# The input half of a GRU's new gate by Strassen's scheme, the state half as loose filler, and a new table of exchanges, on one Trainium2 core

## The chip, the cores and the metric

The kernel runs on one core of one Trainium2 chip. The core has a matrix engine (TensorE, PE in the profile; PEld is its weight load), a vector engine (VectorE, DVE), an activation engine (ScalarE, ACT), GpSimd (POOL) and a sync engine (SyncE, SP). PE multiplies a tile of weights by a tile of data into a PSUM bank; DVE and ACT read and write both PSUM and on-chip memory; SP and POOL issue most of the DMA transfers. Each engine takes its instructions in a fixed order and waits on semaphores. A queue of transfers is held up as well while the transfer at its head waits.

The metric is device time in microseconds (us) for one execution. Before the change: 2009.32 us, the median of three runs (2005.86 to 2010.85).

## The reference, cut to what matters

For 32 graphs of 512 nodes with 256 features everything is float32:

```python
h = max(layernorm(x), 0)                                # per graph [512, 256]
c = relu(bn1(conv1x1(h^T)))                             # 256 -> 256 channels
x_conv = relu(bn2(conv17(c)) + h^T)^T                   # 17 taps along the nodes
s = h @ w_se^T + b_se;  A = exp(-dist(s)) * adj         # [512, 512], s has 3 columns
x_nmp = A @ relu(h @ w_msg^T + b_msg)
gi = [x_conv, x_nmp] @ w_ih^T + b_ih                    # 512 -> 768
gh = h @ w_hh^T + b_hh                                  # 256 -> 768
r = sigmoid(gi_r + gh_r);  z = sigmoid(gi_z + gh_z)
n = tanh(gi_n + r * gh_n)
out = x + (1 - z) * n + z * h
```

The matrix products fill the time: the 17-tap convolution (already turned into 25 smaller products per group of columns by a transform of data and weights), the two products of the graph, and the gate products above. The change is about the gate products, the transform of the convolution's data, and the line with `w_msg` and `w_se`.

## The kernel before, in words

The work is five streams written as Python generators: `rows` (1x1 convolution), `begins` (layer norm and turning of a graph), `graphs` (messages, kernel matrix, masked product), `conv` (the 17-tap convolution in 7 groups of columns, 25 products each) and `gates` (one call of `gates(b)` per graph b). A small planner at the end of the kernel steps the streams. It keeps a model of each engine's time. A stream yields the planner's time at which its next step can go, or a condition; among the streams that can go the planner takes the one that lies furthest behind its share. The table `OTHERS` names choices, by their running number, at which it takes the second or third of the able streams instead. So the order of the instructions on all engines is fixed when the kernel is built, by the planner's constants and by this table. Work for DVE and ACT that isn't urgent goes through `later(t, f)`, a list by due time; `settle()` issues the whole list at once.

All matrix instructions are issued at line 259, all DVE, ACT and most POOL work at line 241, all transfers at line 228. Tiles tell the work apart: `ps_acc` (three PSUM banks) belongs to the gates, `ps_g` to graph and rows, `ps_c` to the convolution.

**The gates before.** For a graph b there are three gates (r, z, n), each with 256 output features in two halves o = 0, 1 of 128. The three data tiles with 2 x 128 input features on the partitions and 512 nodes are `hTb` (state), `xconv` and `xnb` (inputs); each has two buffers. For graphs 1 to 30 the gates r and z are made together by Strassen's scheme in Winograd's form (7 products in place of 8, on half tiles): 2x2 blocks are the two gates by the two halves of input features on one side, and the two halves of 256 nodes on the other. The sums of the weights are made once (`weight_sums`, tiles `wsum`), those of the data per graph by DVE (`data_sums`, tiles `t`). For each o that is 7 products of three sources, each 128 x 256. Two partial results must be copied or added between PSUM banks on the way (ACT's copies, and DVE's adds in `spread`: `ps_acc<-ps_acc,r`, 128 x 256). The new gate isn't in this scheme: per o there are two state products (`hidden`: `ps_acc<-hTb,whh`, 128 x 512) and four input products (`new`, 128 x 512). ACT halves the state part and adds its bias in PSUM, DVE multiplies it there by (tanh + 1) (`ps_acc<-r,ps_acc`), and the input products are then summed on top of it in the same bank. These last products are put into the next unit's waits by `some_new`.

After that comes the mix of a unit: ACT makes n (`r<-ps_acc,vec`), DVE does three operations of 128 x 512 into a tile `o_sb` and `r`, transposes `r` into `o_sb`, and POOL adds `o_sb` onto the output in DRAM by four transfers (`out_dram<-o_sb`). SP has copied x to the output before. Graph 0 and graph 31 (`PLAIN`) are done without the scheme. In the last part of the program, after the other streams have ended, the gates are alone.

**The message step before** (`messages`): per quarter of the nodes one product of 259 columns (256 of `w_msg`, 3 of `w_se`), and two DVE adds that take the bias and leave PSUM, one of 256 and one of 3 columns. `factors` builds from the 3 columns the two small factors of the kernel matrix.

**The transform before** (`fives_alone`): for each group of columns but the first, DVE makes five combinations of the convolution's input in 12 long operations of about 128 x 1632.

## Time and profile before

| | |
|---|---|
| median of 3 runs | 2009.32 us |
| profiled execution, first to last instruction | 2013.5 us |
| PE busy | 1973.8 us, 98% |
| DVE busy | 1505.0 us, 75% |
| ACT busy | 874.1 us, 43% |
| POOL busy | 478.5 us, 24% |
| mean granted clock of PE | 0.991 |
| first gate product, last convolution product, last product outside the gates | 253.5, 1816.4, 1835.1 us |

Each executed float32 product appears in the trace as two matrix instructions, so a count of the trace is twice the count of the program (a few records are missing). The duration of one matrix instruction in the trace holds its way through the array; the pace at which PE goes through them is read from the starts of neighbouring rows. A bracket at the end of a row of the timeline gives the idle time before it and what ended it.

### The profile page before, as it was taken

What the parts mean: (1) busy time and instruction counts of PE and PEld (TensorE: products, weight loads), DVE (VectorE), ACT (ScalarE), POOL (GpSimd) and SP (SyncE); (2) the same over time, 40 slices, a digit from 0 to 9 for tenths busy, and PEclk for the clock granted to TensorE, in tenths of its full rate; (3) what the DMA queues carried; (4) which work ended last, traced back from release to release, by engine and by line L of the source; (5) the groups of instructions that cost most, each with busy time, mean ns of one, the idle gap of its engine ahead of it and who ended that gap; (6) DMA issues with size and microseconds to landing.
All of it is one profiled execution on the core that took longest, in us unless ns stands there. A gap on an engine that the chain in (4) does not pass through costs nothing.

```text
span 2013.5 us, 28526 instructions
## 1 busy us (share of the span) xinstructions
PE 1973.8 (98%) x9692; PEld 1450.8 (72%) x9692; DVE 1505.0 (75%) x2711; ACT 874.1 (43%) x1755; POOL 478.5 (24%) x628
## 2 busy tenths in 40 slices
PE   8999999999999999999999999999999999999998
PEld 5887666776778677776787776777776777776774
DVE  6889589976988597876787775688894877766443
ACT  6644463434634455333464235463334453324321
POOL 3222112222212132222231221232220221113232
PEclk9999899999999999999999999999999999999999
DMA  8446777888898788889787886798895876665564
GB/s 295 168 174 211 238 241 194 211 209 197 227 252 208 194 191 213 200 195 222 146 235 192 204 202 162 191 246 203 179 211 150 185 171 155 157 151 106 111 100 34
DMA packets 578177, 378.92 MB, mean 188 GB/s; under 512 B 457664, under 2 KB 475488, under 8 KB 576896
## 3 DMA queue, kind: packets, MB, share of 16 engines
q1 hardware_dynamic: 419760, 279.15, 49.7%
q0 software_dynamic: 157184, 97.81, 26.4%
q8 instruction: 77, 1.26, 0.2%
q14 instruction: 68, 0.56, 0.1%
q10 hardware_dynamic: 1088, 0.13, 0.0%
HBM read 278.94 MB, written 114.56 MB: 195 GB/s over the span
## 4 chain that ended last, share of the span: by engine, by line
PE 65%; DVE 4%; issue 2%; DMA 1%; ACT 1%; POOL 1%; DVEq 0%; POOLq 0%; SPq 0%; ACTq 0%
PE ps_acc L259 36%; PE ps_c L259 16%; PE ps_g L259 13%; DVE o_sb L241 1%; DMA cd<-part 1%; PE ps_g L265 1%; DVE t L241 0%; POOL out_dram L228 0%; DVE x L241 0%; DMA hd<-hT 0%; POOL cd L228 0%; DVE ps_acc L241 0%; ACT at L241 0%; DVE z L241 0%; DMA w<-wd 0%
## 5 line engine op out<-in xcount | busy, mean ns | idle before, releaser
L228 POOL DMA_DIRECT2D out_dram<-o_sb x252 | 275.8, 1719 | 636.5 <-DVE o_sb L241 510.9
L259 PEld LDWEIGHTS ps_c<-xd,w 128*128 128x128 f32 x2304 | 285.5, 190 | 49.9 <-ACT ps_c L241 33.9
L259 PEld LDWEIGHTS ps_c<-x,w 128*128 128x128 f32 x2032 | 259.8, 194 | 48.2 <-issue 32.9
L259 PE MATMUL ps_c<-xd,w 128*128 128x135 f32 (+1 forms) x2304 | 290.4, 279 | 3.9 <-ACT ps_c L241 3.9
L259 PE MATMUL ps_c<-x,w 128*128 128x135 f32 (+2 forms) x2032 | 268.5, 281 | 2.8 <-DVE x L241 2.8
L259 PE MATMUL ps_g<-at,msg 128*128 128x512 f32 x512 | 230.0, 600 | 3.5 <-DVE at L241 3.5
L241 DVE TENSOR_TENSOR ps_acc<-ps_acc,r 128x256 f32<-128x256 f32 x120 | 51.7, 431 | 230.4 <-PE ps_acc L259 209.3
L259 PE MATMUL ps_acc<-hTb,whh 128*128 128x512 f32 (+2 forms) x532 | 211.4, 495 | 1.4 <-ACT r L241 1.4
L259 PE MATMUL ps_acc<-xconv,wih 128*128 128x512 f32 (+2 forms) x532 | 211.6, 495 | 0.7 <-DVE ps_acc L241 0.7
L259 PE MATMUL ps_acc<-xnb,wih 128*128 128x512 f32 (+2 forms) x532 | 209.1, 496 | 3.2 <-DVE ps_acc L241 3.2
L259 PEld LDWEIGHTS ps_g<-at,msg 128*128 128x128 f32 x512 | 96.9, 193 | 112.8 <-issue 103.4
L259 PE MATMUL ps_acc<-t,wsum 128*128 128x256 f32 x720 | 175.7, 380 | 1.2 <-DVE wsum L241 1.2
L259 PEld LDWEIGHTS ps_acc<-t,wsum 128*128 128x128 f32 x720 | 135.7, 191 | 35.5 <-issue 17.9
L259 PEld LDWEIGHTS ps_acc<-xconv,wih 128*128 128x128 f32 x532 | 98.0, 190 | 48.3 <-issue 38.6
L259 PE MATMUL ps_g<-hT,w 128*128 128x512 f32 (+8 forms) x296 | 124.5, 571 | 7.4 <-DMA hT<-hd 6.8
L259 PEld LDWEIGHTS ps_acc<-xnb,wih 128*128 128x128 f32 x532 | 96.1, 190 | 44.8 <-issue 31.5
L259 PE MATMUL ps_g<-wmsg,hTg 128*128 128x259 f32 x496 | 124.4, 382 | 0.0
L259 PE MATMUL ps_acc<-t,wih 128*128 128x256 f32 x480 | 123.2, 380 | 0.0
L259 PEld LDWEIGHTS ps_acc<-hTb,whh 128*128 128x128 f32 x532 | 94.7, 190 | 38.5 <-issue 28.3
L241 DVE TENSOR_TENSOR x<-x 128x544 f32<-128x544 f32 (+2 forms) x175 | 120.2, 707 | 0.3
L241 ACT ACTIVATE ps_c<-ps_c 128x270 f32<-128x270 f32 (+1 forms) x144 | 56.3, 391 | 137.9 <-PE ps_c L259 137.7
L241 ACT ACTIVATE h<-ps_g,bn_shift,bn_scale 128x252 f32<-128x252 f32 (+8 forms) x212 | 86.3, 484 | 60.4 <-PE ps_g L259 60.4
(157 smaller groups left out, 3251.3 us busy)
## 6 DMA issues: line engine op xcount, KB each, us to landing
w<-wd SPq DMA_DIRECT2D x414, 256.0 KB, 4.0
m_sb<-in_adj_dram SPq DMA_DIRECT2D x384, 64.0 KB, 3.4
wd<-w POOLq DMA_DIRECT2D x74, 256.0 KB, 3.3
hT<-hd SPq DMA_DIRECT2D x33, 512.0 KB, 4.0
hd<-hT POOLq DMA_DIRECT2D x32, 512.0 KB, 6.1
hTb<-hd SPq DMA_DIRECT2D x32, 512.0 KB, 4.6
xnb<-nd SPq DMA_DIRECT2D x64, 256.0 KB, 3.3
out_dram<-o_sb POOLq DMA_DIRECT2D x252, 64.0 KB, 4.8
```

The costliest lines, as they stand in the source:

```text
L228: self.engine.dma_start(dst, src, **more)
L241: getattr(self.engine, op)(*tiles, **more)
L259: nc.tensor.matmul(ps, lhsT, rhs, **more)
L265: nc.tensor.transpose(ps, a, ident)
```

## The change

The change does the following.

- **New gate by the scheme.** For graphs 1 to 30 the input products of the new gate (sources `xconv` and `xnb`) go by the same scheme, with the two halves o = 0, 1 of the outputs as the two block rows. A third run of it follows the two for r and z, with its own sums of weights `nsum`: 7 products of two sources, 128 x 256, in place of 8 products of 128 x 512. All three runs now go through one function, `scheme`.
- **State products as fill-in.** The state products of the new gate are cut into 128 x 256 and put on a list (`state`, `SPARE`), from which `spare_some` takes them into the waits inside a scheme and `spare_all` takes the rest before a scheme's last products. They have a bank of their own. DVE multiplies them by (tanh + 1) into `r`, and a new DVE add (`r<-ps_acc,r`, 128 x 512) joins them with the input products before the tanh.
- **Buffers.** `o_sb` is gone: the mix works in `hTb` itself, so the transfers to the output read `hTb`. `z` has two buffers. Some data sums are made in place in `xconv` and `xnb`, so that these have two DVE operations of 128 x 256 where one of 128 x 512 was.
- **Shorter transform.** `fives_alone` makes its five combinations in 10 long operations in place of 12 (other linear combinations of the same outputs of earlier steps).
- **One message add.** The product has 261 columns (two columns of zeros, so that bias alone gives -0.5), and one DVE add of 261 columns replaces the adds of 256 and 3.
- **Table and constants.** The least time of a matrix product in the planner's model goes from 0.2145 to 0.2235, the gates' starting clock from 1.8 to 2.0, and `OTHERS` is another table: 27 entries before, 205 now.

```diff
-        on_pe(ps, [lhsT, rhs], (0.2675 if few else max(0.2145, 0.005 + elements(ps) / 600.0)) + 0.1 * (few != narrow))
+        on_pe(ps, [lhsT, rhs], (0.2675 if few else max(0.2235, 0.005 + elements(ps) / 600.0)) + 0.1 * (few != narrow))
...
         settle_stores()
+        if ISSUED["out"] < ND * (b - 1):
+            settle()
         HB[b] = late.tile([P, ND, N], F32, name="hTb", bufs=2)
...
         for steps in (
             ((minus, 3, 1),),
-            ((minus, 2, 0), (less2, None, 3), (minus, None, 1)),
-            ((minus, 3, 1), (less2, None, 4), (minus, None, 2)),
-            ((minus, 2, 1), (less2, None, 3), (minus, None, 2)),
-            ((minus, 3, 2), (less2, 1, None)),
+            ((times(2.0), 0, None), (times(-2.0), 2, None)),
+            ((times(-2.0), 3, 4), (times(2.0), 1, None), (minus, None, 2)),
+            ((times(-3.0), 2, 3), (times(2.0), 1, None)),
+            ((minus, 3, 2), (times(-2.0), 1, None)),
         ):
...
-        dve.tensor_tensor(msg[:, c, :], ps[:, :D], bmsg[:, :D], op=ALU.add)
-        dve.tensor_tensor(gr.aug[:, c, :3], ps[:, D:], bmsg[:, D:], op=ALU.add)
+        dve.tensor_tensor(msg[:, c, :], ps, bmsg, op=ALU.add)
...
+            def scheme(ks, given, summed, temp, first, last, over=None):
+                yield bank_read
+                ps0 = acc.tile([P, N], F32, name="ps_acc")
...
+                ps1 = acc.tile([P, N], F32, name="ps_acc")
+                act.activation(ps1[:, lo], ps0[:, lo], AF.Copy)
+                copy_at = act.free + LAG
                 yield now
...
+                term(ps0[:, hi], summed(0), summed_t(0), ks)
+                fifth = temp()
+                act.activation(fifth, ps0[:, hi], AF.Copy)
+                yield from spare_some(copy_at)
                 yield copy_at
+                term(ps1[:, lo], summed(1), summed_t(1), ks)
...
+                dve.tensor_tensor(ps0[:, hi], ps1[:, lo], fifth, op=ALU.add)
+                r_at = dve.free + LAG
                 yield now
+                term(ps0[:, lo], given(1, 0), part_of(1, lo), ks)
+                yield from spare_some(r_at)
                 yield r_at
+                term(ps1[:, lo], given(0, 1), third, ks)
+                dve.tensor_tensor(ps1[:, hi], ps1[:, lo], fifth, op=ALU.add)
+                z_at = dve.free + LAG
...
+                term(ps0[:, hi], summed(2), part_of(1, hi), ks, end=True)
+                first(ps0)
...
+                yield from spare_all()
+                yield max(z_at, *(T_AT[b, 2, k] for k in ks))
+                term(ps1[:, lo], given(1, 1), summed_t(2), ks, end=True)
...
+                last(ps1)
...
+                    def add():
+                        UNREAD.discard(ps.tensor.name)
+                        dve.tensor_tensor(r[o], ps, r[o], op=ALU.add)
+                        later(dve.free + 0.2, squash)
...
+        def make_r(o):
+            settled("mix", ND * (b - 1) + o + 1)
+            r[o] = late.tile([P, N], F32, name="r", bufs=2)
...
     OTHERS = {
-        6: 1, 41: 1, 259: 1, 374: 1, 430: 1, 443: 1, 547: 1, 953: 1, 979: 1, 1020: 2,
...
+        8: 1, 11: 1, 57: 1, 67: 2, 94: 1, 100: 1, 108: 1, 135: 1, 162: 1, 178: 1, 188: 1, 199: 1,
...
```

What the change moves is seen in the order of the built programs. First PE, in the last part of the program where the gates are alone: the new gate's products for o = 0 of graph 29 before (bank 13954; the rows of bank 13979 between them begin the r and z scheme of o = 1).

```order
L259 MATMUL ps_acc_13954<-hTb_13858,whh_2263 128x512 x2
...
L259 MATMUL ps_acc_13979<-hTb_13858,whh_2263 128x256
L259 MATMUL ps_acc_13979<-xconv_13866,wih_2264 128x256
L259 MATMUL ps_acc_13979<-xnb_13813,wih_2264 128x256
L259 MATMUL ps_acc_13954<-xconv_13866,wih_2264 128x512 x2
...
L259 MATMUL ps_acc_13954<-xnb_13813,wih_2264 128x512 x2
```

And the run of the new gate for graph 29 now (banks 14383 and 14386 hold o = 0 and o = 1; 14410 takes the next graph's state products).

```order
L259 MATMUL ps_acc_14383<-xconv_14201,wih_2238 128x256
L259 MATMUL ps_acc_14383<-xnb_14242,wih_2238 128x256
L259 MATMUL ps_acc_14383<-t1_0_2246,nsum_2242 128x256
L259 MATMUL ps_acc_14383<-t2_0_2249,nsum_2242 128x256
L259 MATMUL ps_acc_14386<-t1_1_2247,nsum_2242 128x256
L259 MATMUL ps_acc_14386<-t2_1_2250,nsum_2242 128x256
...
L259 MATMUL ps_acc_14383<-xconv_14201,nsum_2242 128x256
L259 MATMUL ps_acc_14383<-xnb_14242,nsum_2242 128x256
L259 MATMUL ps_acc_14410<-hTb_14336,whh_2237 128x256 x4
L259 MATMUL ps_acc_14386<-t1_2_2248,wih_2238 128x256
L259 MATMUL ps_acc_14386<-t2_2_2251,wih_2238 128x256
```

Twelve products of 128 x 512 per graph have become 14 of 128 x 256 and 8 of 128 x 256, and in this part the state products all stand just before the last two products of a run.

Second DVE, at the step from graph 28 to graph 29 in the same part, before: the mix of one unit, the data sums of the next graph among it, up to the step on which the waiting input products rest (`ps_acc<-r,ps_acc`).

```order
L241 TENSOR_TENSOR o_sb_13891<-hTb_13739,r_13827 128x512
L241 SCALAR_TENSOR_TENSOR o_sb_13891<-z_13851,o_sb_13891 128x512
L241 SCALAR_TENSOR_TENSOR r_13827<-o_sb_13891,r_13827 128x512
L241 TENSOR_TENSOR t0_0_2268<-hTb_13858 128x512
L241 TENSOR_TENSOR t2_0_2274<-xnb_13813 128x512
L241 STREAM_TRANSPOSE o_sb_13891<-r_13827 128x512
L241 TENSOR_TENSOR t1_0_2271<-xconv_13866 128x512
L241 TENSOR_TENSOR t2_1_2275<-xnb_13813,t2_0_2274 128x256
L241 SCALAR_TENSOR_TENSOR ps_acc_13901<-r_13881,ps_acc_13901 128x512
```

The same step now: the last two data sums for graph 29, the add of o = 1, the mixes of both units of graph 28 one after the other, both transposes, and then the first add between banks of graph 29's first run.

```order
L241 TENSOR_TENSOR t1_2_2248<-xconv_14201,t1_1_2247 128x256
L241 TENSOR_TENSOR t2_2_2251<-xnb_14242,t2_1_2250 128x256
L241 TENSOR_TENSOR r_14212<-ps_acc_14249,r_14212 128x512
L241 TENSOR_TENSOR hTb_14062<-hTb_14062,r_14176 128x512
L241 SCALAR_TENSOR_TENSOR hTb_14062<-z_14196,hTb_14062 128x512
L241 SCALAR_TENSOR_TENSOR r_14176<-hTb_14062,r_14176 128x512
L241 TENSOR_TENSOR hTb_14062<-hTb_14062,r_14212 128x512
L241 SCALAR_TENSOR_TENSOR hTb_14062<-z_14238,hTb_14062 128x512
L241 SCALAR_TENSOR_TENSOR r_14212<-hTb_14062,r_14212 128x512
L241 STREAM_TRANSPOSE hTb_14062<-r_14176 128x512
L241 STREAM_TRANSPOSE hTb_14062<-r_14212 128x512
L241 TENSOR_TENSOR ps_acc_14286<-ps_acc_14294,r_14313 128x256
```

Both units' mixes and transposes now stand on DVE ahead of the next graph's first add between banks; before, one unit's mix stood there and the other's came a unit later.

Third SP, in the middle of the program: the loads around the state tile of graph 19, `hTb_11023`, now (the `w` tiles are the convolution's weights, `xconv` the same graph's convolution result).

```order
L228 DMA w_11011<-wd14_282 128x512
L228 DMA w_11013<-wd14_282 128x512
L228 DMA hTb_11023<-hd19_96 128x1024
L228 DMA xconv_11025<-cd19_152 128x1024
L228 DMA w_11037<-wd15_283 128x512
```

The load of `hTb` stands in SP's queue with the convolution's weights behind it, as before; what it must wait for is new, since the buffer that it fills is read by the transfers of graph 17's output.

More of the change, by code (lines that the diff above doesn't have):

```diff
@@ new lines, with hidden_half, hide_some, run @@
+    ISSUED = {"mix": 0, "out": 0}
+    UNREAD, STATE, SPARE, HIDE, R_AT = set(), {}, [], [], {}
+    def hidden_half(ps, o, s=slice(0, N)):
+        act.activation(ps[:, s], ps[:, s], AF.Identity, bias=bn[:, o : o + 1], scale=0.5)
+    def hide_some():
+        def run():
+            while HIDE and HIDE[0][:2] in STATE:
+                HIDE.pop(0)[2]()
+        later(act.free + 0.3, run)
+    def state(b, o):
+        def one(n):
+            i, half = divmod(n, 2)
+            if n == 0:
+                ps = STATE_PS[b, o] = acc.tile([P, N], F32, name="ps_acc")
+                UNREAD.add(ps.tensor.name)
+            ps = STATE_PS[b, o]
+            at = slice(HALF * half, HALF * half + HALF)
+            matmul(
+                ps[:, at], whh[:, i, 2 * D + o * P : 2 * D + (o + 1) * P], HB[b][:, i, at],
+                start=(n == 0), stop=(i == ND - 1), skip_group_check=True,
+            )
+            if n == 2 * ND - 1:
+                hidden_half(ps, o)
+                STATE[b, o] = ps
+                hide_some()
+        SPARE.extend((b, lambda n=n: one(n)) for n in range(2 * ND))
```

601 lines of the change are left out of this document (289 added, 312 removed), and 21 rows, old and new, of the table OTHERS.

## The prediction

> **What bounds the kernel now.** I read the page's busy times first, then PE's busy time by stage, then what stands in PE's way in the last stage.
>
> ```profile
> PE 1973.8 (98%) x9692; PEld 1450.8 (72%) x9692; DVE 1505.0 (75%) x2711; ACT 874.1 (43%) x1755; POOL 478.5 (24%) x628
> ```
>
> ```profile
> 0.00:60.00 60.00, 52.94 (x206) 33.43 (x207) 38.93 (x121) 38.58 (x84) 17.02 (x41) 0.94 0.71 261
> 60.00:340.00 280.00, 271.39 (x1599) 204.60 (x1598) 230.97 (x422) 140.37 (x304) 62.08 (x108) 0.98 0.67 210
> 340.00:1000.00 660.00, 651.42 (x3243) 483.18 (x3242) 531.11 (x946) 290.99 (x601) 152.97 (x197) 0.99 0.84 204
> 1000.00:1700.00 700.00, 694.10 (x3393) 517.17 (x3392) 531.60 (x931) 305.70 (x594) 163.52 (x200) 1.00 0.81 192
> 1700.00:1843.00 143.00, 141.93 (x689) 105.54 (x688) 102.16 (x169) 47.05 (x97) 30.67 (x32) 1.00 0.65 140
> 1843.00:2013.50 170.50, 162.04 (x572) 106.91 (x570) 70.21 (x125) 51.37 (x78) 52.20 (x52) 0.99 0.57 90
> ```
>
> The rows give stage, length, then busy time of PE, PEld, DVE, ACT, POOL, and PE's clock. PE is the bound in every stage: it idles 31.2 us in the first 1843 us (7.1 + 8.6 + 8.6 + 5.9 + 1.1) and 8.5 us in the last stage, most of these after its last product. So work taken off PE is time, as long as the new order doesn't open waits.
>
> The last stage is different in kind. From 1843 us the gates are alone, and no other stream fills a wait. Its chain of waits, in order of time:
>
> ```profile
> 1886.80 23.14 PE ps_acc L259 x86
> ...
> 1910.30 0.69 DVE o_sb L241
> ...
> 1912.35 1.29 DVE t L241 x2
> ...
> 1915.16 0.61 DVE ps_acc L241
> 1915.82 23.13 PE ps_acc L259 x86
> ```
>
> Once per graph (1886.80 to 1915.82: 29.02 us) the chain leaves PE and goes through 5.5 us on DVE (1910.30 to 1915.82), the mix of the finished unit with data sums in between, until DVE gives PE a bank back. PE's own rows show how much of this isn't covered:
>
> ```profile
> 1857.77 1.98 PE L259 MATMUL ps_acc<-xnb,wih 128*128 128x512 f32 x4 [0.98 <-DVE ps_acc L241]
> 1886.80 1.99 PE L259 MATMUL ps_acc<-xnb,wih 128*128 128x512 f32 x4 [0.30 <-DVE ps_acc L241]
> ...
> 1944.85 1.98 PE L259 MATMUL ps_acc<-xnb,wih 128*128 128x512 f32 x4 [0.30 <-DVE ps_acc L241]
> ```
>
> **The change part by part.** *Products.* The pace of PE:
>
> ```profile
> 1960.91 1.46 PE L259 MATMUL ps_acc<-t,wsum 128*128 128x256 f32 x6
> 1962.20 0.60 PE L259 MATMUL ps_acc<-hTb,whh 128*128 128x256 f32 x2
> ...
> 1976.06 3.60 PE L259 MATMUL ps_acc<-hTb,whh 128*128 128x512 f32 x8
> 1979.49 1.88 PE L259 MATMUL ps_acc<-xconv,wih 128*128 128x512 f32 x4
> ```
>
> Six instructions of 256 columns take 1.29 us from start to start, so a product (two instructions) takes 0.430 us; eight of 512 take 3.43 us, 0.8575 us a product. A graph's new gate goes from 12 x 0.8575 = 10.29 us to 22 x 0.430 = 9.46 us. Over 30 graphs that is 360 x 0.8575 - 660 x 0.430 = 308.7 - 283.8 = 24.9 us less. The messages' 256 products get two more columns of 0.43/256 us each: +0.9 us. Together **-24.0 us** of PE work, all of it on the path.
>
> *DVE and ACT.* Row by row:
>
> ```profile
> L241 DVE TENSOR_TENSOR ps_acc<-ps_acc,r 128x256 f32<-128x256 f32 x120 | 51.7, 431 | 230.4 <-PE ps_acc L259 209.3 <-ACT r L241 11.5 <-PE ps_g L265 5.1
> L241 DVE SCALAR_TENSOR_TENSOR ps_acc<-r,ps_acc 128x512 f32<-128x512 f32 x63 | 43.4, 689 | 17.0 <-ACT r L241 12.8 <-ACT ps_acc L241 4.2
> L241 DVE TENSOR_TENSOR t<-xconv,t 128x256 f32<-128x256 f32 x60 | 25.0, 416 | 0.0
> L241 DVE TENSOR_TENSOR t<-xconv 128x512 f32<-128x512 f32 x30 | 20.1, 670 | 0.0
> L241 DVE TENSOR_TENSOR aug<-ps_g,bmsg 128x3 f32<-128x3 f32 x128 | 19.3, 151 | 0.0
> L241 DVE TENSOR_TENSOR x<-x,h 128x1632 f32<-128x1632 f32 x12 | 22.3, 1855 | 0.2
> ```
>
> Added: 60 adds between banks (60 x 0.431 = 25.9 us), 60 joins `r<-ps_acc,r` (no such row; nearest is the multiply that also reads a bank, 0.689: 41.3 us), and 60 sums of 512 columns become 120 of 256 (60 x (2 x 0.416 - 0.670) = 9.7 us). Removed: 128 adds of 3 columns (19.3 us), and 2 long operations in each of 6 groups (12 x 1.855 = 22.3 us). DVE gains about 35 us, 1505 to 1540, and ACT 60 copies of 0.38 us. Both stay below PE, so in the first 1843 us I cost them at nothing: the planner sees their backlog and gives PE another stream's products meanwhile. If that cover were gone, the 35 us would be an upper price.
>
> *The last stage.* There the cover is gone, and I follow the step from one graph to the next in the order that the change builds. Time 0 is the end of graph b's last product. DVE may write the last two data sums of graph b+1 only then, since that product reads their old contents; the starts of DVE's rows at this place before give the paces:
>
> ```profile
> 1911.01 0.69 DVE L241 SCALAR_TENSOR_TENSOR o_sb<-z,o_sb 128x512 f32<-128x512 f32 x1
> 1911.74 0.69 DVE L241 SCALAR_TENSOR_TENSOR r<-o_sb,r 128x512 f32<-128x512 f32 x1
> 1912.35 0.69 DVE L241 TENSOR_TENSOR t<-hTb 128x512 f32<-128x512 f32 x1
> ...
> 1916.01 0.42 DVE L241 TENSOR_TENSOR t<-xnb,t 128x256 f32<-128x256 f32 x1
> 1916.35 0.42 DVE L241 TENSOR_TENSOR t<-xconv,t 128x256 f32<-128x256 f32 x1
> ```
>
> 0.34 us for a sum of 256, 0.73 for an operation of 512 that needs the one before it, 0.61 for one that doesn't. So: the sums from 0.15 on, the join for o = 1 at 0.83, the first mix at 1.44, 2.17, 2.90, the second at 3.51, 4.24, 4.97, the transposes at 5.58 and 6.2, and only then, at 6.8, the first add between banks of graph b+1, done by 7.25. PE reaches the product that needs this add's bank after 12 products, at 12 x 0.430 = 5.16 us. It waits about 2.1 us. Four such steps have nothing but gates around them (into graphs 27 to 30): +8.4 us, and the four waits above (0.98 once and 0.30 three times, 1.9 us) go: **+6.5 us**. Ends: -1.9 if DVE gets through in time after all, +13.3 if each wait also costs a window of half clock (below).
>
> The clock is what makes a wait dear elsewhere:
>
> ```profile
> 198.00:202.40 4.40, 1.47 (x6) 0.82 (x5) 4.23 (x13) 0.00 (x0) 0.00 (x0) 1.00 0.74 230
> 202.40:205.80 3.40, 3.40 (x6) 1.34 (x5) 0.57 (x1) 0.87 (x2) 0.00 (x0) 0.50 0.92 292
> ```
>
> ```profile
> 201.76 4.51 PE L259 MATMUL ps_g<-hT,w 128*128 128x512 f32 x6 [2.94 <-DMA hT<-hd]
> 455.69 6.71 PE L259 MATMUL ps_g<-hT,w 128*128 128x512 f32 x8 [2.33 <-DMA hT<-hd]
> 174.07 3.80 PE L259 MATMUL ps_c<-x,w 128*128 128x116 f32 x32 [1.75 <-DVE x L241]
> ```
>
> After the wait of 2.94 us PE's clock is halved for 3.4 us, which costs 1.7 us more (the last column of a stage row but two is the clock); after the one of 1.75 us the trace shows no half clock. The wait of 2.1 us that I expect lies between them, nearer the harmless one, so I take no clock loss. The Trainium skill ("TensorE: Matmul & The Clock Gate", Part 1) says that the gate goes back to half rate after at least one idle window of about 3.4 us; by that rule none of the four waits could halve the clock, while the trace's 2.94 us already did. By the rule the term stays +6.5, with the loss it would be +13.3.
>
> *The table.* The order of the first 1843 us is drawn anew. Its 31.2 us of idle PE bound the gain; a third more of it, 10 us, is my bound for a loss. The two waits for `hT<-hd` above, with a half window behind the first and two behind the second (3.4/2 + 6.8/2), are worth 10.4 us and belong to this order alone; the new order loses them and draws others. I take a little under half: **-4 us**.
>
> The sum: -24.0 + 6.5 - 4.0 = -21.5 us. The profiled execution spans 2013.5 us, 4.2 over the median, and would come to 1992; of the runs' median, 2009.3, **1988 us** is left.
>
> **The rivals.** *The last stage runs through.* DVE is in time there and the table gains more (-24.0 - 1.9 - 8): 1975 us. For it: DVE is busy only 70 of the last 170.5 us. Against it: the chain above already runs through DVE once per graph, with less in the way.
>
> *The gain goes into new waits in the middle.* Each graph has three runs with two hand-overs to ACT and two to DVE each, where it had two; if each of 26 graphs in the middle waits once more, as long as the longest wait above (0.98 us), that is +25 us against the table's -4: 2009.3 - 24.0 + 6.5 + 25 - 4 = 2013, and with half of it 2000. For it: DVE is 80% busy from 340 to 1000 us (531 of 660). Against it: in the same stage PE now loses only 1.3%.
>
> *SP is held by the state tile.* This is the way to a slower kernel.
>
> ```profile
> 1943.57 4.33 POOL L228 DMA_DIRECT2D out_dram<-o_sb x4 [11.43 <-DVE o_sb L241]
> ```
> ```profile
> out_dram<-o_sb POOLq DMA_DIRECT2D x252, 64.0 KB, 4.8
> ```
> ```profile
> SPq L228 <- PE ps_c L259: 445.8, 200, 11.3
> ```
> ```profile
> L259 PE MATMUL ps_c<-xd,w x2304: 276/279/384, 249.9 to 1816.4; 128*128 128x135 f32 x128, 128*128 128x136 f32 x64
> ```
>
> The load of `hTb` for graph b+1 fills the buffer that eight output transfers of graph b-1 read. POOL needs 2 x 4.33 us to issue them, and the last lands some 4.8 us after its issue began; with about 6 us of mix that is 19 us after graph b-1's last product, and the load stands in SP's queue after graph b's first run, 21 products or 9.0 us of PE work, some 17 us where the gates have about half of PE. So SP may stand for a few us, with the weights of the convolution behind it. They have slack: SP waits 445.8 us in all for PE to free their buffers, 2.2 us each time. It decides from the point where SP stands longer than a convolution product's period: the 150 of groups 2 to 7 lie between 250 and 1816 us, 10.4 us each; 1.5 us over that in 27 graphs would be +40: 2028 us. Against it: that needs twice the hold that I work out.
>
> *Half clock in the last stage.* Four windows, +6.8: 1995 us, still faster. *The products don't get cheaper*: excluded by the pace rows; 256 columns cost half of 512.
>
> **How the numbers follow.** The forecast (1980 to 1997) has 0.55, the last stage that runs through 0.15, waits in the middle 0.16, SP's hold 0.07, the half clock 0.07. The range takes the forecast's, most of the faster rival and the milder half of the waits: 1973 to 2005 us. A measurement of this kernel can tell 0.3%, 6 us, from no change. Faster, below 2003.3: 0.55 + 0.15 + 0.07 + a third of the waits' 0.16 = 0.82; the same 0.11; slower, above 2015.3, 0.07.
>
> **What would show it.** PE's busy time falls by 20 to 26 us. In the last stage the period of a graph is 29.5 to 30 us (27.6 of products), and PE's row of `ps_acc<-t,whh` in a run's fifth group carries a wait of about 2 us put down to DVE `ps_acc`. DVE is near 1540 us. PE's idle time before that stage is 20 to 35 us. I'd be wrong if the period there is near 27.7 (no wait), if PE waits for weights `w<-wd` in the middle (SP's hold), or if DVE's waits appear all over the middle.

## The result, and the profile after

The change makes the kernel slower: **2145.9 us** (median of 4 runs, 2141.2 to 2152.2) against 2007.6 us (4 runs) for the kernel before on the same chip, a ratio of 1.070 (95% interval 1.067 to 1.073). The prediction was 1988 us. Its profiled execution spans 2150.4 us, 136.9 more than before.

PE is still the engine with the most to do, but it no longer has a busy line without holes. The page's busy times:

```profile
PE 1996.3 (93%) x10291; PEld 1564.9 (73%) x10291; DVE 1549.5 (72%) x2747; ACT 896.3 (42%) x1815; POOL 474.9 (22%) x629
```

PE idles 154.1 us of the span, where it idled 39.7 us. By stage (columns as in the prediction: stretch, length, then busy time of PE, PEld, DVE, ACT, POOL, and PE's clock):

```profile
340.00:1000.00 660.00, 617.04 (x3262) 488.08 (x3259) 514.92 (x904) 288.38 (x599) 136.92 (x185) 0.99 0.80 198
1000.00:1700.00 700.00, 648.02 (x3310) 518.95 (x3310) 503.71 (x871) 287.91 (x567) 152.38 (x191) 0.98 0.77 179
1943.00:2150.40 207.40, 176.84 (x699) 133.05 (x697) 84.12 (x156) 53.52 (x88) 55.62 (x54) 0.96 0.51 79
```

From 340 to 1700 us PE idled 14.5 us before and idles 94.9 us now. That is where other streams have work, and where the forecast counted on no waits. The view of what PE waited for (us in total, times, longest us) names two rows that hold 125 us of it:

```profile
PE ps_acc L259 <- ACT ps_acc L241: 69.0, 68, 10.3
PE ps_acc L259 <- DVE ps_acc L241: 56.0, 55, 3.4
PE ps_g L259 <- DMA hT<-hd: 3.5, 3, 2.1
```

Before, all rows of this view came to 33.1 us and the row for DVE `ps_acc` to 4.2 us; now they come to 146.9. The groups of instructions by line (the last columns are the idle time just before a group and what ended it) tell which products stand behind these waits:

```profile
L259 PE MATMUL ps_acc<-hTb,whh 128*128 128x256 f32 x720 | 200.2, 391 | 36.5 <-DVE ps_acc L241 36.4
L259 PE MATMUL ps_acc<-t,wsum 128*128 128x256 f32 x720 | 178.4, 390 | 50.3 <-ACT ps_acc L241 50.3
L259 PE MATMUL ps_acc<-xconv,wih 128*128 128x256 f32 x540 | 166.5, 390 | 19.6 <-DVE ps_acc L241 19.6
L259 PE MATMUL ps_acc<-t,nsum 128*128 128x256 f32 x240 | 63.5, 401 | 18.7 <-ACT ps_acc L241 18.7
```

`t,wsum` and `t,nsum` begin the second group of a run of `scheme`, `hTb,whh` and (in the run of the new gate) `xconv,wih` the fourth. So it is not the fifth group that waits, the one that the prediction spoke of. One step of the last stage in order of time, rows of PE, ACT and DVE:

```profile
2046.55 0.43 DVE L241 TENSOR_TENSOR t<-xconv,t 128x256 f32<-128x256 f32 x1 [0.40 <-PE ps_acc L259]
...
2046.78 0.59 PE L259 MATMUL ps_acc<-hTb,whh 128*128 128x256 f32 x2
...
2047.32 0.68 DVE L241 TENSOR_TENSOR r<-ps_acc,r 128x512 f32<-128x512 f32 x1
...
2047.64 0.59 PE L259 MATMUL ps_acc<-xnb,wih 128*128 128x256 f32 x2
2047.92 0.68 DVE L241 TENSOR_TENSOR hTb<-hTb,r 128x512 f32<-128x512 f32 x1
2048.27 0.37 ACT L241 ACTIVATE ps_acc<-ps_acc 128x256 f32<-128x256 f32 x1 [0.80 <-PE ps_acc L259]
...
2048.69 2.86 PE L259 MATMUL ps_acc<-t,wsum 128*128 128x256 f32 x12 [0.46 <-ACT ps_acc L241]
...
2052.03 1.30 DVE L241 STREAM_TRANSPOSE hTb<-r 128x512 f32<-128x512 f32 x2
2052.82 0.38 ACT L241 ACTIVATE r<-ps_acc 128x256 f32<-128x256 f32 x1 [3.56 <-DVE hTb L241]
...
2053.25 0.43 DVE L241 TENSOR_TENSOR ps_acc<-ps_acc,r 128x256 f32<-128x256 f32 x1
...
2053.73 0.70 PE L259 MATMUL ps_acc<-hTb,whh 128*128 128x256 f32 x2 [2.18 <-DVE ps_acc L241]
...
2054.26 0.59 PE L259 MATMUL ps_acc<-xconv,wih 128*128 128x256 f32 x2
...
2054.70 0.59 PE L259 MATMUL ps_acc<-xnb,wih 128*128 128x256 f32 x2
...
2060.93 2.86 PE L259 MATMUL ps_acc<-t,wsum 128*128 128x256 f32 x12 [0.46 <-ACT ps_acc L241]
...
2064.38 0.70 PE L259 MATMUL ps_acc<-hTb,whh 128*128 128x256 f32 x2 [0.59 <-DVE ps_acc L241]
```

The first group ends in the left half of a bank. ACT copies that half into another bank (2048.27 to 2048.64), and only then PE goes on, though its next product needs nothing of the copy: it writes the right half of the same bank. The second wait is the same with DVE: the add writes the right half (2053.25 to 2053.68), and the product behind it, whose sum goes into the left half, starts at 2053.73. In the program's list of PE's instructions both products carry a wait, one for ACT and one for DVE. Here are the second to fourth group of a run late in the program, of the change and of the kernel before (numbers of tiles left out):

```
change                                  before
ps_acc<-t_0,wsum [waits Activation]     ps_acc<-t_0,wsum [waits Activation]
ps_acc<-t_0,wsum                        ps_acc<-t_0,wsum
ps_acc<-t_0,wsum                        ps_acc<-t_0,wsum
ps_acc<-t_1,wsum [waits DVE]            ps_acc<-hTb,whh
ps_acc<-t_1,wsum                        ps_acc<-xconv,wih
ps_acc<-t_1,wsum                        ps_acc<-xnb,wih [waits DMAHW0]
ps_acc<-hTb,whh [waits DVE]             ps_acc<-t_1,wsum [waits DVE,PE]
ps_acc<-xconv,wih                       ps_acc<-t_1,wsum [waits DVE]
ps_acc<-xnb,wih                         ps_acc<-t_1,wsum
```

Before, the product of the left half came ahead of ACT's second copy and of the add, so it had nothing to wait for. The wait for ACT's first copy was there as well, but new-gate products from a list stood between the first group and the second. In the trace of the kernel before, same place in the last stage:

```profile
1914.92 0.59 PE L259 MATMUL ps_acc<-xnb,wih 128*128 128x256 f32 x2
1915.82 1.98 PE L259 MATMUL ps_acc<-xnb,wih 128*128 128x512 f32 x4 [0.30 <-DVE ps_acc L241]
1917.64 1.88 PE L259 MATMUL ps_acc<-xconv,wih 128*128 128x512 f32 x4
1919.36 1.46 PE L259 MATMUL ps_acc<-t,wsum 128*128 128x256 f32 x6
```

The rows of the trace leave the numbers of the tiles out. Laid beside the program's list, which has them, no row of PE in the whole trace of the change overlaps in time with a row of ACT or DVE on the same PSUM tile. The Trainium skill ("PSUM — Partial Sum Buffer", section "PSUM bank collisions raise a hardware error") says that two engines may not touch the same bank in the same partitions at once, at disjoint columns either, and that the compiler's scheduler therefore puts a dependency between them. The trace agrees with the dependency; what would happen without it was not tried.

The price of such a hand-over, from the rows: where nothing waits, pairs start 0.43 to 0.44 us apart (2054.26, 2054.70). From 2047.64 to 2048.69 are 1.05 us, 0.62 more. The wait in the bracket is 0.46 of it; the rest is the way of PE's last product out of the array before ACT can begin. The first pair after a wait takes 0.10 us more (2053.73 to 2054.26: 0.53). A copy thus costs 0.72 us. From 2060.93 to 2064.38 are 3.45 us for six products (2.58), 0.10 of the excess from the wait ahead of them; with the pair behind it the add costs 0.87 us.

Not every hand-over costs only that. In the last stage the bare wait is 0.46 us for a copy and 0.59 us for an add. Cut at these two lengths, the 123 waits of the two rows hold 63 us; the other 62 us are time in which ACT or DVE, busy with other work, came late to the copy or add (the longest wait is 10.3 us). This split is an estimate from the single waits of the two rows.

### The profile page after: what moved, and what is told of

It is laid out like the page before. It is cut to its first block, busy times and chain, and to the rows that moved or that the text cites. A ratio compares the mean times of both kernels' runs of the same rounds, so it can differ in the third digit from the quotient of the medians.

```text
span 2150.4 us, 29846 instructions
## 1 busy us (share of the span) xinstructions
PE 1996.3 (93%) x10291; PEld 1564.9 (73%) x10291; DVE 1549.5 (72%) x2747; ACT 896.3 (42%) x1815; POOL 474.9 (22%) x629
## 5 line engine op out<-in xcount | busy, mean ns | idle before, releaser
L228 POOL DMA_DIRECT2D out_dram<-hTb x240 | 264.6, 2145 | 422.7 <-DVE hTb L241 401.2
L259 PE MATMUL ps_acc<-hTb,whh 128*128 128x256 f32 (+2 forms) x772 | 222.3, 403 | 36.5 <-DVE ps_acc L241 36.4
L259 PE MATMUL ps_acc<-xconv,wih 128*128 128x256 f32 (+2 forms) x592 | 189.4, 406 | 19.6 <-DVE ps_acc L241 19.6
L259 PEld LDWEIGHTS ps_acc<-hTb,whh 128*128 128x128 f32 x772 | 138.5, 192 | 80.8 <-DVE ps_acc L241 51.3
L259 PE MATMUL ps_acc<-xnb,wih 128*128 128x256 f32 (+2 forms) x592 | 187.1, 402 | 0.0
L259 PEld LDWEIGHTS ps_acc<-xconv,wih 128*128 128x128 f32 x592 | 110.6, 194 | 54.6 <-DVE ps_acc L241 28.1
L259 PEld LDWEIGHTS ps_acc<-xnb,wih 128*128 128x128 f32 x592 | 112.9, 194 | 23.6 <-issue 9.1
L259 PE MATMUL ps_g<-wmsg,hTg 128*128 128x261 f32 x496 | 124.9, 383 | 0.0
L241 DVE TENSOR_TENSOR msg<-ps_g,bmsg 128x261 f32<-128x261 f32 x128 | 53.7, 424 | 88.0 <-PE ps_g L259 86.7
L241 ACT ACTIVATE r<-ps_acc,brz 128x512 f32<-128x512 f32 x64 | 44.0, 688 | 162.9 <-PE ps_acc L259 147.4
```

The source lines that it names most:

```text
L228: self.engine.dma_start(dst, src, **more)
L241: getattr(self.engine, op)(*tiles, **more)
L259: nc.tensor.matmul(ps, lhsT, rhs, **more)
```

## The experiments

The theory (A): the order of groups inside a run makes PE hand a bank to ACT and to DVE and stand until it comes back, six times per graph. The planner counts a PSUM bank by columns, so it sees no wait and gives PE nothing else. The rivals: (B) the new table of exchanges drew a bad order; (C) DVE and ACT simply have more to do. All medians below are beside runs of the kernel before on the same chip (2006.0 to 2007.6 us).

| kernel | median us | ratio to before (95%) | PE's waits, us (times) | mean clock |
|---|---|---|---|---|
| before | 2007.6 | 1 | 33.1 (42) | 0.991 |
| the change | 2145.9 | 1.067 to 1.073 | 146.9 (148) | 0.983 |
| gives way first, both | 2086.0 | 1.036 to 1.042 | 95.5 (82) | 0.985 |
| gives way first, copy only | 2143.0 | 1.065 to 1.071 | 129.6 (109) | 0.978 |
| gives way first, add only | 2157.2 | 1.073 to 1.076 | 148.1 (124) | 0.972 |
| old group order | 2080.5 | 1.035 to 1.040 | 92.3 (91) | 0.987 |
| the change, no table | 2186.0 | 1.086 to 1.093 | 168.7 (167) | 0.975 |
| old group order, no table | 2103.3 | 1.046 to 1.050 | 107.1 (91) | 0.982 |
| before, no table | 2060.1 | 1.023 to 1.029 | 64.8 (65) | 0.983 |
| old group order, asks for a free bank | 2055.1 | 1.022 to 1.026 | 72.0 (79) | 0.987 |
| same, table found for it | 2032.1 | 1.011 to 1.015 | 55.3 (72) | 0.992 |
| same, another table | 2030.3 | 1.009 to 1.013 | 61.6 (74) | 0.991 |
| the change, banks counted whole | 2177.5 | 1.083 to 1.087 | 177.8 (181) | 0.989 |
| before, transform and one add | 2028.3 | 1.007 to 1.012 | 42.2 (46) | 0.995 |

PE's waits are the sum of all rows of the view of what PE waited for, from one profiled execution each.

### Giving way before the waiting group

```diff
-                term(ps0[:, hi], summed(0), summed_t(0), ks)
-                fifth = temp()
-                act.activation(fifth, ps0[:, hi], AF.Copy)
                 yield from spare_some(copy_at)
                 yield copy_at
+                term(ps0[:, hi], summed(0), summed_t(0), ks)
+                fifth = temp()
+                act.activation(fifth, ps0[:, hi], AF.Copy)
                 term(ps1[:, lo], summed(1), summed_t(1), ks)
...
-                term(ps0[:, lo], given(1, 0), part_of(1, lo), ks)
                 yield from spare_some(r_at)
                 yield r_at
+                term(ps0[:, lo], given(1, 0), part_of(1, lo), ks)
```

> Edit: in the function scheme the stream gives way to the planner before the second group instead of after it (until ACT's copy is done), and before the fourth group instead of after it (until DVE's add is done). The same products, copies and adds in the same order within a run; nothing else. Theory A (PSUM hand-overs: PE stands because the second group writes the bank that ACT is just copying from, and the fourth the bank that DVE is just adding into, and the planner does not know of these waits): the two rows of PE's waits that hold 69.0 us (ACT ps_acc) and 56.0 us (DVE ps_acc) fall together from 125 to under 50 us, since other streams' products now stand there in the first 1850 us; the time falls by 80 to 110 us, to 2035 to 2065. In the last stage, where nothing else is there to fill, the period of a graph stays 33 to 34.5 us. Rival B (the new table of exchanges drew a bad order; the waits are where it left them): the table now meets other choices, so the time moves by less than 20 us either way, and the waits go elsewhere but keep a sum above 100 us. Rival C (DVE and ACT have more to do, and PE waits for their backlog wherever it comes): same DVE and ACT work, so the sum of waits stays above 120 us and the time within 2125 to 2160.

Measured: 2086.0 us, 60 less than the change. The two rows fell from 125 to 34 us, and new ones came up:

```profile
PE ps_acc L259 <- DVE ps_acc L241: 19.4, 11, 3.7
PE ps_acc L259 <- ACT ps_acc L241: 14.4, 17, 4.0
PE ps_acc L259 <- DVE r L241: 13.8, 9, 3.5
PE ps_c L259 <- ACT n L241: 12.0, 4, 5.1
PE ps_c L259 <- ACT z L241: 12.0, 6, 5.8
```

The direction is A's, since only the place where the stream gives way was moved, and B (under 20 us either way) and C (above 2125 us) are both missed; the time misses A's range by 21 us as well, because 91 us of waits left and 40 us of others came. The last stage was misjudged: its period fell to 30.9 us, since the state products that stand ready as fill-in now take part of the waits there.

### Each half alone

> Edit: of the first experiment only the first half: the stream gives way before the second group (ACT's copy); the fourth group stands where the change has it, right behind DVE's add. Theory A (each hand-over of a bank has its own price): PE's waits put down to ACT ps_acc fall from 69 to under 25 us, those put down to DVE ps_acc stay at 45 to 65 us; the time lies between the change's 2146 and the 2086 of the run that has both halves: 2105 to 2130. Rival (one of the two alone does the harm, or any other order under this table would do as well): the time is within 10 us of 2086, and DVE's row falls too; or within 10 us of 2146 with ACT's row gone.

> Edit: the counterpart of the run with the copy alone: only the second half of the first experiment, the stream gives way before the fourth group (DVE's add); the second group stands where the change has it. The copy alone gave 3 us of the 60 us that both gave. If the two are additive, this one gives the other 57: 2080 to 2100 us, with PE's waits for DVE ps_acc under 25 us and those for ACT ps_acc at 60 to 80. Rival (the two aren't additive: a hand-over that is left draws the waits of the mended one to itself, since PE meets ACT or DVE late again at the next group): 2115 to 2150, with ACT's row above 75 us.

The copy alone: 2143.0 us. The add alone: 2157.2 us, slower than the change. Their rows of waits, the copy alone first:

```profile
PE ps_acc L259 <- DVE ps_acc L241: 60.9, 48, 4.9
PE ps_acc L259 <- ACT ps_acc L241: 13.6, 15, 2.9
PE ps_g L259 <- DMA hT<-hd: 12.1, 6, 5.4
```

```profile
PE ps_acc L259 <- ACT ps_acc L241: 97.6, 78, 5.8
PE ps_acc L259 <- DVE ps_acc L241: 18.8, 11, 5.4
```

Each mended hand-over lost its row, as expected, but the time hardly moved or rose: the other hand-over's row kept its size or grew (56.0 to 60.9; 69.0 to 97.6), other rows came up, and the clock fell (0.978 and 0.972; at half clock for 96 and 123 us, against 76 in the change). The theory that the two prices add up falls: 3 and -11 us against 60. The second run's rival had the rows right (ACT's above 75 us), though the time is 7 us above its range. What the rows show is that a mended wait alone wasn't a gain here: PE arrived at the next thing that wasn't ready. Both runs also keep the table made for the change's own order, and what that hides isn't known, so why a half doesn't pay stays open.

### The old order of groups, and the tables

```diff
-                term(ps0[:, hi], summed(0), summed_t(0), ks)
-                fifth = temp()
-                act.activation(fifth, ps0[:, hi], AF.Copy)
                 yield from spare_some(copy_at)
                 yield copy_at
+                term(ps0[:, hi], summed(0), summed_t(0), ks)
+                term(ps0[:, lo], given(1, 0), part_of(1, lo), ks)
                 term(ps1[:, lo], summed(1), summed_t(1), ks)
+                fifth = temp()
+                act.activation(fifth, ps0[:, hi], AF.Copy)
...
-                term(ps0[:, lo], given(1, 0), part_of(1, lo), ks)
```

> Edit: as the kernel before orders its groups: the stream gives way until ACT's copy is done, then the second, fourth and third group are issued, then ACT's second copy and DVE's add, and the stream gives way until that add is done; the rest as in the change. The same products, copies and adds, another order. Theory A: PE never writes a bank that ACT or DVE is working on, apart from true needs; PE's waits put down to ACT and DVE ps_acc fall from 125 to under 35 us, and the time to 2000 to 2035. In the last stage the period falls from 34.0 to 29.5 to 31 us, with one wait of about 2 us, now ahead of the fifth group. Rival B (table): within 20 us of the change, 2125 to 2165. Rival C (backlog of DVE and ACT): within 2125 to 2160, and the last stage keeps its period near 34.

> Edit: the change with its table of 205 exchanges left empty; all else as it is. Theory A: the waits are in the order inside a run of the scheme, which no exchange of streams can take apart: the waits put down to ACT and DVE ps_acc stay between 100 and 150 us, and the time is 2140 to 2190 (an order without any table costs something more elsewhere). Rival B (the new table is the cause): the time falls by over 40 us, below 2105. Rival C: 2130 to 2180, no better told from A here.

> Edit: the old order of the groups (as in the run above that has it) and an empty table. Shows the group order's worth without any table, against the change with an empty table. Theory A: faster than the change with an empty table by 90 to 140 us, at 2010 to 2060; waits put down to ACT and DVE ps_acc under 40 us. Rivals B and C: within 25 us of the change with an empty table.

> Edit: the kernel before with its table of 27 exchanges left empty. Shows what a table found for a kernel is worth, and so how much of the 70 to 95 us that still lie between the runs with mended group order and the kernel before can be the want of a fitting table. Theory A1 (a table is worth some 20 us, the rest of the gap is another wait of the new scheme): 2015 to 2040. Rival B1 (the whole rest is the table): 2070 or more.

With the old group order 2080.5 us, 65 less than the change; with an empty table on both sides 2103.3 against 2186.0, 83 less. So the order of a few lines inside a run is worth 65 to 83 us, with the change's table and with none, and PE's waits for ACT and DVE `ps_acc` fall to 31 us, as A had it (under 35). B and C, which expected at most 25 us, fall for this part. Something of C is left: ACT and DVE come late to many hand-overs (the 62 us above), but in the old group order, with the same work, PE hardly stands for them. How much belongs to the groups and how much to the place where the stream gives way isn't separated: the first experiment kept the change's groups and had 60 us, and its four runs (2077.8 to 2089.0) overlap with these (2077.3 to 2084.2). In the last stage the period is 30.7 us, and its waits have shrunk to these:

```profile
1976.93 1.13 PE L259 MATMUL ps_acc<-t,wih 128*128 128x256 f32 x4 [0.69 <-DVE ps_acc L241]
...
1980.01 1.56 PE L259 MATMUL ps_acc<-t,wsum 128*128 128x256 f32 x6 [0.46 <-ACT ps_acc L241]
...
1984.93 0.70 PE L259 MATMUL ps_acc<-t,whh 128*128 128x256 f32 x2 [0.77 <-DVE ps_acc L241]
```

A's range (2000 to 2035) was missed again, and without tables it was missed too: 83 us where A had 90 to 140, and 2103 us where it had 2010 to 2060. The change without its table came out as A said (2140 to 2190 us, the two rows at 134 us). The run of the kernel before without its table points to what A left out: 2060.1 us, 53 more than with it, outside what either theory expected. A fitting table is worth 53 us to the kernel before and 40 us to the change. Of the 138 us that the change lost, 126 are there without any table (2186.0 against 2060.1), so the two tables account for about 12 us. Any edit that shifts the running number of the choices throws that away, so an edited kernel with a table made for another order must be compared with others that have none: 2103.3 against 2060.1, 43 us, is what all the rest of the change still costs in the old group order, as far as one order of each can tell.

### Asking whether the bank is free

In the old group order a row of the groups by line points to the three banks, since this product is also the one that opens a bank (a run's first group, and the state products), and DVE's reading of the state sums (`r`) and ACT's of z end the use of one:

```profile
L259 PE MATMUL ps_acc<-hTb,whh 128*128 128x256 f32 x720 | 201.0, 386 | 13.0 <-DVE r L241 7.4 <-ACT z L241 5.5
```

The experiment lets the stream give way until the bank is free, and the planner counts banks whole (two lines more, so that line 259 is 261 there):

```diff
+        if a.tensor.name.startswith("ps_"):
+            return 0, P, 0, 4 * N
...
                 yield bank_read
+                yield acc.free("ps_acc")
                 ps0 = acc.tile([P, N], F32, name="ps_acc")
```

> Edit: the run with the old group order, and two things more: the stream gives way at the start of a run of the scheme until the bank that its first group takes is free by the planner's count (in the change it asks only whether the bank's reader has been issued), and the planner counts a PSUM bank as one piece, not by columns. Theory A2 (what is left is of the same kind: the planner sends PE to a bank that DVE or ACT still holds; three banks must now carry the state's sums beside a run's two): PE's waits put down to DVE r and to ACT and DVE ps_acc fall together from 39 us to under 22 us, and the time from 2080 to 2035 to 2065. Rival C2 (what is left is plain backlog on DVE and ACT, which have more to do per graph): the waits go to other rows and the time stays within 10 us of 2080.

Measured: 2055.1 us, 25 less, in A2's range of time; the rows named there came to 38.3 us (14.7, 13.1 and 10.5), not under 22. So the time is as A2 said and its account isn't: the rows that shrank are those of `ps_c` behind ACT (25.3 us in the run before this one, 12.3 here). What part of the 25 us is the asking and what part another draw of the order stays open.

Counting whole banks without a new group order is the counterpart:

> Edit: the change as it is (its group order, its table), only that the planner counts a PSUM bank as one piece, not by columns, and so knows of the waits. Theory A (the order inside a run, where the stream gives way only behind the group that must wait, fixes them; knowing of them moves other streams' products but not these): PE's waits put down to ACT and DVE ps_acc keep 100 to 140 us, and the time 2120 to 2170. Rival B2 (the planner's blind spot alone is the cause, the group order would do): below 2100.

```profile
PE ps_acc L261 <- ACT ps_acc L243: 90.6, 79, 7.1
PE ps_acc L261 <- DVE ps_acc L243: 60.5, 66, 3.5
```

2177.5 us: the planner knows of the waits and can't do anything about them, because the stream gives way only behind the group that waits. That is 7.5 us above A's range, and the rows are higher than expected too (151 us). Rival B2, the blind spot alone, falls. The order inside a run, of the groups and of the place where the stream gives way, is the cause of the largest part of the loss, and the blind spot is what hid it from the planner.

### A table for the mended order

> Edit: the run that asks for a free bank (old group order, PSUM counted by whole banks, the stream gives way until its bank is free, now also for the bank of the state products), and a table of exchanges found anew for this order. Theory A (what was left of the loss, some 50 us, is the want of a fitting table, as the kernel before loses 54 us without its own; the change's lighter products then show): 1995 to 2018 us, the kernel before or a little under it; PE's waits in all under 55 us, half of the 92 of the run with the old group order alone. Rival C3 (the new scheme itself costs some 40 us that no order takes away): 2035 or more.

> Edit: as the run beside it, with a second table found separately. Theory A: 1995 to 2018 us, within 10 us of the other table's; so it is the order of groups and the asking for banks that lets a table work, not one lucky table. Rival C3: 2035 or more.

2032.1 and 2030.3 us, 12 to 14 above A's range and 3 to 5 below where C3 began. So a fitted table (and asking for the state products' bank too) gave 23 to 25 us, and two tables found separately agree within 2 us. PE's page line and the longest rows of waits of the first one:

```profile
PE 1959.9 (97%) x10291; PEld 1556.3 (77%) x10291; DVE 1546.6 (76%) x2747; ACT 892.2 (44%) x1815; POOL 473.8 (23%) x629
```

```profile
PE ps_acc L261 <- DVE ps_acc L243: 9.9, 15, 1.3
PE ps_g L261 <- DMA hT<-hd: 9.8, 7, 3.4
PE ps_acc L261 <- ACT ps_acc L243: 7.2, 15, 1.0
```

Of the 138 us that the change lost, 114 are back. PE's busy time is 13.9 us under that of the kernel before, and still no run beats it: the execution spans 2023.4 us, 9.9 more than before, with 63.5 us of idle PE against 39.7. Why this order keeps more idle time is open. The rows before offer one reason that wasn't tried: the kernel before has new-gate products of 0.8575 us, eight per graph, to put where a run waits (1915.82 to 1919.36 above), and the change has turned these into a run with hand-overs of its own and left eight state products of 0.430 us as fill-in.

### The small parts

The kernel before with the shorter transform, the one message add and the planner's 0.2235:

> Edit: the kernel before with the change's shorter transform, its one message add (with the two columns of zeros) and its planner's time of 0.2235 for a matrix product; gates, buffers and table as before. Theory: DVE's busy time falls by 35 to 45 us (1505 to about 1465), and the time moves by less than 12 us either way (1996 to 2020), since DVE isn't the bound and the table now meets other choices: the loss of the change is not in these parts. Rival: one of these parts (or the planner's constant) costs, 2030 or more.

DVE's busy time fell by 33 us (1505.0 to 1471.8), a little less than expected. The time rose by 22 us, 8 above the range, with PE's waits 9 us higher. It lies well inside what the lost fit of the table can cost (53 us), so it tells only that these parts don't account for 138 us; what they are worth with a table of their own isn't known.

## Why the prediction was wrong, point by point

**Products: right.** The pace is as predicted (pairs 0.43 to 0.44 us apart), so the -24.0 us of PE work are real. They can't be read from PE's busy time, which rose by 22.5 us in place of falling by 20 to 26: each wait adds to it the way of the product ahead out of the array (0.16 us) and 0.10 us for the pair behind, and the clock went from 0.991 to 0.983, which over the spans costs 18 us before and 37 after. As an estimate from these figures, 106 more waits at 0.26 us and 19 us of clock, less the 24.0, come to 22.6 us. With the order mended and a table found for it, PE's busy time is 13.9 us under that of the kernel before.

**"In the first 1843 us I cost them at nothing: the planner sees their backlog": this is the step that failed.** The amounts were nearly right (DVE 1549.5 us, 1540 predicted; ACT 22 us more). What was missed isn't their amount but where PE stands while they work. The planner doesn't see a copy or an add that shares only a bank with the next product. So the cover wasn't there, and the price wasn't the 35 us of added work but 125 us of waits in two rows. The rival of the waits in the middle was the right one. It counted the hand-overs, but gave them one wait of 0.98 us per graph, 25 us in all, where each graph has six that PE stands for: 180 in 30 graphs, of which 123 show a wait, of 1.02 us on average.

**The last stage: right in kind, with two errors.** DVE's list was right to 0.1 us. Counted from the first sum (2046.55), the join was forecast at 0.68 and stands at 0.77, the first mix at 1.29 and 1.37, the transposes at 5.43 and 5.48, the add's end at 7.10 and 7.13. Wrong was "PE reaches the product that needs this add's bank after 12 products": it stops after 9, ahead of the fourth group. And a graph has more hand-overs than the one. From the rows: PE begins the run at 2046.78 and goes on at 2053.73, 6.95 us later, with 9 x 0.430 = 3.87 us done: 3.08 late, the first copy within it, and 0.10 for the pair behind. The two other copies cost 0.72 each, the two other adds 0.87. 27.6 + 3.08 + 0.10 + 1.44 + 1.74 = 34.0 us, and from one wait of 2.18 to the next (2019.76 to 2053.73) the trace has 34.0. The forecast was 29.5 to 30. That the wait for DVE's add has nearly the forecast length (2.18 and 2.1 us) is chance: PE stops for it three products early, and 0.72 us late by then from the copy.

**The clock.** For the wait of 2.1 us no loss was taken, and there is none at 2053.73. But the last section shows equal waits with one and what it hangs on, which the forecast didn't ask, so this step was right by luck.

**The table.** Costed at -4, with +10 as the worst. The bound was taken from the idle time that the old table left, not from what stands without one. A table is worth 40 to 53 us here, more than any term of the sum; only because the new one is worth nearly as much as the old does the difference, some 12 us of loss, come near the bound.

**The other rivals.** SP is held, as that rival said:

```profile
SPq L228 <- DMA out_dram<-hTb: 275.3, 43, 39.6
```

That is 6.4 us each time, but the view of PE's waits has no row for the loading of the convolution's weights, so the hold didn't reach PE by that way. This rival named the right sign for a reason that isn't there.

## What to carry to other kernels

Before costing a copy or an add between PSUM banks at nothing, look at which product is issued next: if it writes the same bank, at whatever columns, PE stands until the other engine is done, and the wait belongs to the order inside the stream, where no planner can fill it unless the stream gives way ahead of that product. Order the groups so that those of a bank are all done before another engine gets it, or give way first; here either gave back 60 us or more. And where a kernel's order comes from a found table, compare edits with the table emptied on both sides, or with one found for each; otherwise the lost fit (53 us here) hides what the edit does.

## What the runs showed that was not expected

The same wait can leave the clock alone or halve it. The change's last stage has the same wait ahead of the fourth group in each of its steps, 34 to 36 us apart; three of them, and the stage row behind the first:

```profile
1984.10 1.02 PE L259 MATMUL ps_acc<-hTb,whh 128*128 128x256 f32 x2 [2.17 <-DVE ps_acc L241]
...
2019.76 0.70 PE L259 MATMUL ps_acc<-hTb,whh 128*128 128x256 f32 x2 [2.18 <-DVE ps_acc L241]
...
2053.73 0.70 PE L259 MATMUL ps_acc<-hTb,whh 128*128 128x256 f32 x2 [2.18 <-DVE ps_acc L241]
```

```profile
1984.20:1987.70 3.50, 3.50 (x9) 2.76 (x10) 0.00 (x0) 0.00 (x0) 3.50 (x7) 0.52 0.91 43
```

At 1984.10 the pair takes 1.02 us and the clock is halved for 3.4 us, at the other two it isn't. In the kernel that mends the add alone each of the four waits of 2.18 us halves it; one step, and the stage row behind it:

```profile
2031.83 1.11 PE L259 MATMUL ps_acc<-hTb,whh 128*128 128x256 f32 x2 [2.18 <-DVE ps_acc L241]
```

```profile
2031.90:2035.30 3.40, 3.40 (x9) 2.69 (x10) 0.00 (x0) 0.00 (x0) 3.40 (x7) 0.51 0.95 45
```

So the length of a single wait doesn't decide. Where it lies does. In each trace here the stretches of half clock all begin on one grid with steps of 3.413 us, to within 0.003 us; in the change 1984.34 is a point of it. The wait that ends at 1984.10 lies whole inside one step, and the one that ends at 2019.76 is cut in two by the point at 2018.47. The rows of these steps (PE's busy time stands behind the length):

```profile
1980.93:1984.34 3.41, 1.24 (x6) 0.78 (x5) 3.04 (x6) 0.38 (x1) 0.94 (x2) 1.00 0.00 0
2015.06:2018.47 3.41, 2.52 (x12) 1.88 (x10) 3.31 (x6) 0.23 (x1) 0.00 (x0) 1.00 0.00 0
2018.47:2021.89 3.42, 2.13 (x10) 1.90 (x11) 1.23 (x3) 0.38 (x1) 2.60 (x4) 1.00 0.39 22
```

PE idles 2.17 us of the first step, and 0.89 and 1.29 us of the other two. Counted from 250 us on over all 14 traces, 125 steps that ran at full clock hold 2.0 us of idle PE or more, and half clock follows every one of them; of the 7196 with less it follows 36, some of them with hardly any idle time, so idle time isn't the only way to it. In the kernel that mends the add alone, the steps of the last stage lie 34.0 us apart, close to ten steps of the grid, so that the wait stays inside one step of it each time. The Trainium skill ("TensorE: Matmul & The Clock Gate", Part 1) speaks of at least one idle window of about 3.4 us. The stretches of half clock are that long here and so are the steps of the grid, but a step needn't be idle throughout: 2.0 us of idle time in it were enough, and here the measurement decides. What sets off the other 36 isn't settled.
